# Linear attention with routed experts on one core: rows of tokens through the gate and up products in pairs, four places per pair for the attention's steps, loop transfers on GpSimd

## The chip, the cores and the metric

The kernel runs on one core of a Trainium2 chip. The metric is the device time of one execution, in microseconds; the time before is the median of three runs. Beside these there is one profiled execution, whose records all views of the profile come from.

## What is computed

The input x has 8 sequences of 1024 tokens with 256 features; everything is float32. After a layer norm without weights, two branches are added to x:

```python
q, k, v = (xn @ W.T for W in (Wq, Wk, Wv))          # 16 heads of 16
q, k = elu(q) + 1, elu(k) + 1
kv_cumsum = cumsum(einsum('blhd,blhe->blhde', k, v), axis=1)
out = einsum('blhd,blhde->blhe', q, kv_cumsum)
out = out / clip(einsum('blhd,blhd->blh', q, cumsum(k, axis=1)), 1e-6)
attn = out.reshape(8, 1024, 256) @ Wo.T

logits = xn @ Wr + br                                # 8 experts
w, e = top_k(logits, 2);  w = softmax(w)
h = silu(xn @ W1[e]) * (xn @ W3[e])                  # 256 -> 512
ffn = sum over the two experts of w * (h @ W2[e])    # 512 -> 256
result = x + attn + ffn
```

## The kernel before

The 8192 tokens are 16 blocks of 512. The kernel has three strands of work, written into one program.

**Routing.** Each block is loaded (`load_x`, tile xb), normalised, turned so that features lie on partitions (`turn`, tile xnT, stored to xnT_d in DRAM for the attention), and multiplied by Wr. Every four blocks `route` finds the two best experts of each token and the token's place in its expert's list. From the lists come 128-token rows, each of one expert: `first_batch` makes 25 rows (N1) from the first four blocks, `second_batch` makes 110 more (N2) when all blocks are routed. Each batch yields a table with the expert of each row (te_i), the token numbers to gather (src_i), and the numbers of the table entries (num_i). Of the 135 rows the last three (NR) run only if they are needed; 132 are run by the loop.

**Experts.** For one row j: `ffn_load` gathers its 128 tokens (tile xg) and their weights and norm factors (tile entry) with two indirect transfers on GpSimd; `ffn_weights` reads the expert's number into a register of SyncE and loads W1 and W3 of that expert, 512 KB each (tile w13; its pool has 5 buffers); `ffn_norm` normalises on ScalarE; `ffn_turn` transposes on TensorE into PSUM (xg_t) and copies to xgT; `ffn_hidden` does the gate and up products, each 4 x 2 products of 128 x 128 weights with 128 columns of tokens, into two PSUM tiles gu_ps; a Silu on ScalarE (L1147) and a product on VectorE (L1150) make hT; `ffn_out` multiplies with W2 (y_ps, 256 columns) and scales (L1165); `ffn_store` adds the result into DRAM with an indirect transfer. In float32 the profile shows each product as two records.

**Attention.** `block_steps` cuts each block into 11 steps: projections (zq, zkk, zkv), transposes of k (tp) and the running sum ksum on VectorE, the denominators (den, then two reciprocals on VectorE, L843), and for each of four chunks of 128 tokens the scores (s_ps, four PSUM tiles at once; masked on VectorE, L872), the state update (kv_ps), the weighting (o_ps) and the output projection (a_ps). `attend_upto(n)` advances this strand until n steps are made.

The loop runs over the rows. One pass of it: normalise row j + 1; in the first 12 passes route another block, whose transfers (load_x, and the store of xnT in `turn`) stand on ScalarE's queue; then `attend_upto`; then `ffn_step(j)`, which issues loads for rows ahead, does `ffn_hidden(j)`, `ffn_turn(j + 1)`, `ffn_out(j - 1)`, and the store. So the attention's steps, about 1.4 for a row in the late part, stand in one place per row, between the y products of one row and the gate products of the next.

Four PSUM tiles (pool ps_mm) serve zq, zkk, zkv, den, s_ps and gu_ps; two (ps_t) serve xg_t, tp, kv_ps and o_ps; two (ps_y) serve y_ps and a_ps. After the start, whose order is written out by hand, a scheduler puts the instructions of each engine into an order by its own estimate of times; the order of the built program can be read without running it.

Of the kernel before, what the change touches and what calls it, by code (L numbers as in the profile page):

```python
# [47 lines left out]
I32 = mybir.dt.int32  # L48
# [14 lines left out]
def tile_attention_moe(  # L63
# [33 lines left out]
    NM = NF - NR  # L97
    assert N2 <= P and N1 <= 32 and 2 * FT * N1 + 32 <= KC * TB
# [214 lines left out]
    def turn(t):  # L313
        xn = scaled.pop(t)
        if 0 < t < FB:
            xnT = e_one.tile([P, KC, TB], F32, name=f"xnT{t}")
        else:
            xnT = (two if t == 0 else f_two).tile([P, KC, TB], F32, tag="xnT", name="xnT")
        for k in range(KC):
            tp = ps_t.tile([P, TB], F32, tag="t", name="tp")  # L320
            for c in range(NCH):
                done = nc.tensor.transpose(
                    tp[:, bass.ts(c, P)], xn[:, c, bass.ts(k, P)], ident
                )
                if t == FB + 1:
                    in_order(done)
            nc.scalar.copy(xnT[:, k, :], tp)
        if t == 0:
            turned_first.append(xnT)
        else:  # L330
            last_store[0] = nc.scalar.dma_start(out=xnT_d[t], in_=xnT.rearrange("p k l -> p (k l)"))
        turned[t] = xnT
# [197 lines left out]
    def rows_of(past, jumps, room, start, n, name):  # L530


        nc.vector.tensor_tensor(
            jumps, past, room.unsqueeze(1).to_broadcast([P, n, E - 1]), ALU.mult
        )
        rows = f_one.tile([P, n], F32, name=name)
        nc.vector.tensor_reduce(rows, jumps, op=ALU.add, axis=AX.X)
        if start is None:
            nc.vector.tensor_tensor(rows, rows, cols[:, 0:n], ALU.add)
        else:  # L540
            nc.vector.scalar_tensor_tensor(
                rows, rows, start, cols[:, 0:n], ALU.add, ALU.add
            )
        return rows
# [53 lines left out]
    def first_batch():  # L598
# [17 lines left out]
        past = past_experts(upto, N1, e_one, "past")  # L616
        taken = f_one.tile([P, E], F32, name="taken")
# [7 lines left out]
        rows = rows_of(past, jumps, room, None, N1, "rows1")  # L625
# [15 lines left out]
        for j in range(2):  # L641
            for a in range(0, FT, PART):
                if j == 1 and a >= late:
                    at = late_at[(a - late) // PART]
                else:
                    at = at_places(place, j, a)
                for i in range(PART):
                    c = N1 * (j * FT + a + i)
                    nc.tensor.matmul(
                        sum_ps[32 * i : 32 * i + 32, :], lhsT=marks[:, c : c + 32],  # L650
                        rhs=at[:, i, :], start=(j + a == 0), stop=(j == 1 and a == FT - PART),
                        skip_group_check=True,
                    )
                if j == 0 and a == 2 * PART:
                    _, te_i = numbers_of(past, N1, "1")
            if j == 0:
                yield
# [9 lines left out]
    def second_batch(taken):  # L667
# [4 lines left out]
        upto = add_up(left, "upto2")  # L672
        past = past_experts(upto, N2, f_x, "xb")
        te, te_i = numbers_of(past, N2, "2")
        nc.vector.tensor_copy(rows_left, upto[0:1, E - 1 : E])

        room = f_one.tile([P, E - 1], F32, name="room2")
        nc.vector.tensor_scalar(
            room, rows[:, 0 : E - 1], -1.0, float(ROWS), ALU.mult, ALU.add
        )  # L680
        nc.vector.tensor_tensor(room, room, taken[:, 1:E], ALU.add)
        of_tiles = rows_of(past, past, room, taken[:, 0:1], N2, "rows2")
# [384 lines left out]
    ffn5 = ctx.enter_context(tc.tile_pool(name="ffn5", bufs=5))  # L1067
    ffn4 = ctx.enter_context(tc.tile_pool(name="ffn4", bufs=4))
    ffn8 = ctx.enter_context(tc.tile_pool(name="ffn8", bufs=8))
# [12 lines left out]
    def ffn_load(j):  # L1082
        table, _, num_i, src_i, _, _, i = of_tile(j)
        xg[j] = ffn4.tile([P, H], F32, tag="xg", name="xg")
        nc.gpsimd.indirect_dma_start(  # L1085
            out=xg[j], out_offset=None, in_=x_rows[:, :],
            in_offset=bass.IndirectOffsetOnAxis(ap=src_i[:, i : i + 1], axis=0),
        )
        entry[j] = ffn8.tile([P, 3], F32, tag="entry", name="entry")
        nc.gpsimd.indirect_dma_start(  # L1090
            out=entry[j], out_offset=None, in_=table[:, :],
            in_offset=bass.IndirectOffsetOnAxis(ap=num_i[:, i : i + 1], axis=0),
        )

    def ffn_norm(j):
        in_order(
            nc.scalar.activation(  # L1097
                xg[j], xg[j], AF.Identity, bias=entry[j][:, 1:2], scale=entry[j][:, 2:3]
            )
        )  # L1100

    def ffn_turn(j):

        tp = ps_t.tile([P, KC, P], F32, tag="t", name="xg_t")
        for k in range(KC):
            nc.tensor.transpose(tp[:, k, :], xg.get(j)[:, bass.ts(k, P)], ident)  # L1106
        xgT[j] = ffn2.tile([P, KC, P], F32, tag="xgT", name="xgT")
        nc.scalar.copy(xgT[j], tp)  # L1108
# [8 lines left out]
    def ffn_weights(j):  # L1117
        e = expert_of(j, mybir.EngineType.SP)
        for s, w in enumerate((w1, w3)):
            ws[j, s] = ffn5.tile([P, KC, I], F32, tag="w13", name="w13")  # L1120
            in_order(
                nc.sync.dma_start(
                    out=ws[j, s],
# [4 lines left out]
    def ffn_hidden(j, last=False):  # L1128


        gu = []
        for s in range(2):
            if last and s == 1:
                ffn_out(j - 1, True)
            w13 = ws.pop((j, s))
            ps = ps_mm.tile([P, IC, P], F32, tag="mm", name="gu_ps")
            for i in range(IC):
                for k in range(KC):
                    done = nc.tensor.matmul(  # L1139
                        ps[:, i, :], lhsT=w13[:, k, bass.ts(i, P)], rhs=xgT[j][:, k, :],  # L1140
                        start=(k == 0), stop=(k == KC - 1),
                    )
                    if last:
                        in_order(done)
            gu.append(ps)
        hT = ffn2.tile([P, IC, P], F32, tag="hT", name="hT")
        silu = nc.scalar.activation(hT, gu[0], AF.Silu)  # L1147
        if j == 0:
            in_order(silu)
        nc.vector.tensor_tensor(hT, gu[1], hT, ALU.mult)  # L1150
        hs[j] = hT

    def ffn_out(j, last=False):
        hT = hs.pop(j)
        e = expert_of(j, mybir.EngineType.PE)
        y_ps = ps_y.tile([P, H], F32, tag="y", name="y_ps")
        for i in range(IC):
            done = nc.tensor.matmul(  # L1158
                y_ps, lhsT=hT[:, i, :], rhs=w2_sb[:, bass.ds(e * (IC * H) + i * H, H)],
                start=(i == 0), stop=(i == IC - 1),  # L1160
            )
            if last:
                in_order(done)
        ys[j] = ffn5.tile([P, H], F32, tag="y", name="y")
        nc.vector.tensor_scalar(ys[j], y_ps, entry.pop(j)[:, 0:1], None, ALU.mult)  # L1165

    def ffn_store(j):
        _, _, _, _, rows, dst_i, i = of_tile(j)
        nc.gpsimd.indirect_dma_start(  # L1169
            out=rows[:, :],  # L1170
            out_offset=bass.IndirectOffsetOnAxis(ap=dst_i[:, i : i + 1], axis=0),
            in_=ys.pop(j), in_offset=None, compute_op=ALU.add,
        )

    stored = [0]

    def ffn_step(j, behind):


        if j + 3 < NM:  # L1180
            ffn_load(j + 3)
        if j + 2 < NM:
            ffn_weights(j + 2)
        if j < NM:
            ffn_hidden(j, j == NM - 1)
        if j + 1 < NM:
            ffn_turn(j + 1)
        if j > 0 and j != NM - 1:
            ffn_out(j - 1)
        for _ in range(2):  # L1190
            if stored[0] < j - behind:
                ffn_store(stored[0])
                stored[0] += 1


    for j in range(3):
        ffn_load(j)
    for j in range(2):
# [5 lines left out]
    LATE = 3  # L1204
# [3 lines left out]
    for j in range(NM + 1):  # L1208
        if j + 1 < NM:
# [5 lines left out]
        if j == 0:  # L1215
            for i in range(3, 6):
                load_x(t + i, nc.scalar)
        if 0 < j and t < NBLK:
# [6 lines left out]
            if t + 5 < NBLK:  # L1225
                load_x(t + 5, nc.scalar)
# [15 lines left out]
        if LISTS <= j < LISTS + NBLK - FB:  # L1242
            t = FB + j - LISTS
            rows = slice(t * TB, (t + 1) * TB)
            in_order(nc.sync.dma_start(out=out_rows[rows, :], in_=x_rows[rows, :]))
        if j < LISTS:
            attend_upto(3 + j // 2)
        elif j < READ:
            attend_upto(AHEAD - 2 * (READ - j - 1))
        else:  # L1250
            attend_upto(AHEAD + (NBLK * STEPS - AHEAD) * (j - READ + 1) // (NM - READ - 4))
# [3 lines left out]
        ffn_step(j, LATE if N1 < j <= N1 + LATE else 0)  # L1255
    while stored[0] < NM:
# [6 lines left out]
    with tc.If(used > N2 - NR):  # L1263
        for j in range(NM, NF):
            ffn_load(j)
# [3 lines left out]
            ffn_hidden(j)  # L1269
# [39 lines left out]
```

## Time and profile before

| | us |
|---|---|
| median of three runs | 1396.2 |
| lowest and highest | 1394.3, 1397.18 |
| profiled execution | 1388.92 |
| its span, first to last instruction | 1387.1 |
| TensorE (PE) busy in the span | 1328.5 |
| VectorE (DVE) busy | 728.0 |
| ScalarE (ACT) busy | 488.7 |
| GpSimd (POOL) busy | 528.3 |

The profiled execution is 7.3 us shorter than the median. Busy time is the time in which at least one instruction of the engine runs; PE is TensorE's products, PEld its weight loads, SP the engine that issues most transfers. In lists of groups and waits a line such as L1139 is the line of the kernel, "out<-in" are the program's tiles, and x is a count. A wait is written as "who, line <- whom, line: us in total, times, longest". In timelines the columns are start, duration, engine, line, operation, tiles, count, and in brackets the idle time before it and what ended it.

### The profile page before, as it was taken

The numbers are of one execution on the slowest core, as the hardware profiler recorded it, in microseconds if no ns is written. First come the engines' busy times: TensorE is split into PE (matmuls) and PEld (weight loads), VectorE is DVE, ScalarE is ACT, GpSimd is POOL, SyncE is SP. The second block draws the span as 40 slices with busy tenths as digits, with TensorE's granted clock in tenths as the row PEclk, the third lists the DMA queues.
The fourth block names the chain that finished last, engine by engine and source line by source line (L and its number), as shares of the span: only waits on it lengthen the run. The fifth ranks groups of instructions, "written<-read, shape, count | busy, mean of one in ns | idle before, by whom it ended". The sixth has DMA issues, their size and how long they took to land.

```text
span 1387.1 us, 27907 instructions
## 1 busy us (share of the span) xinstructions
PE 1328.5 (96%) x10906; PEld 1127.2 (81%) x10906; DVE 728.0 (52%) x1428; ACT 488.7 (35%) x914; POOL 528.3 (38%) x457
## 2 busy tenths in 40 slices
PE   5799999999999999999999999999999999999996
PEld 4578887878888888888888888888788788888895
DVE  7786589784353536354453536363544435363631
ACT  5466351141514233252525142342524151423321
POOL 3533332223334333434433333443434244334432
PEclk9999999999999999999999999999999999999999
DMA  9687653455756555555656555565647375555553
GB/s 346 236 275 234 180 169 109 120 143 145 211 160 152 164 124 145 150 145 151 152 147 164 147 151 152 140 173 139 162 129 175 109 173 160 132 164 138 147 151 80
DMA packets 129412, 223.56 MB, mean 161 GB/s; under 512 B 14818, under 2 KB 53346, under 8 KB 128994
## 3 DMA queue, kind: packets, MB, share of 16 engines
q1 hardware_dynamic: 84306, 165.95, 36.9%
q0 software_dynamic: 38064, 43.22, 19.3%
q10 hardware_dynamic: 6912, 12.58, 2.5%
q8 instruction: 90, 1.47, 0.4%
q14 instruction: 40, 0.33, 0.1%
HBM read 187.91 MB, written 44.29 MB: 167 GB/s over the span
## 4 chain that ended last, share of the span: by engine, by line
PE 82%; DVE 11%; ACT 3%; issue 2%; DMA 2%; POOL 0%; POOLq 0%; ACTq 0%; DVEq 0%
PE gu_ps L1139 32%; PE y_ps L1158 15%; PE s_ps L865 6%; PE o_ps L906 4%; PE a_ps L928 4%; PE zq L764 4%; PE zkk L780 3%; PE zkv L780 3%; PE kv_ps L880 2%; DVE rden L843 2%; PE xg_t L1106 2%; PE held_ps L696 2%; PE o_ps L899 2%; PE den L842 2%; DVE ksum L832 2%
## 5 line engine op out<-in xcount | busy, mean ns | idle before, releaser
L1139 PEld LDWEIGHTS gu_ps<-xgT,w 128*128 128x128 f32 x4224 | 494.7, 193 | 28.8 <-issue 17.2
L1139 PE MATMUL gu_ps<-xgT,w 128*128 128x128 f32 x4224 | 511.6, 278 | 2.3 <-DVE s_sb L872 1.9
L1085 POOL DMA_INDIRECT xg<-in_x_dram,src_i x132 | 129.8, 983 | 547.7 <-ACT xgT L1108 437.8
L1158 PE MATMUL y_ps<-w_sb,hT 128*128 x1056 | 251.9, 380 | 2.5 <-DVE hT L1150 1.3
L1169 POOL DMA_INDIRECT out_dram<-y,dst_i x107 | 173.6, 1622 | 159.4 <-DVE y L1165 85.1
L1150 DVE TENSOR_TENSOR hT<-gu_ps,hT 128x512 f32<-128x512 f32 x132 | 90.4, 685 | 248.2 <-PE gu_ps L1139 229.2
L1147 ACT ACTIVATE hT<-gu_ps 128x512 f32<-128x512 f32 x132 | 78.8, 597 | 381.1 <-PE gu_ps L1139 380.2
L1158 PEld LDWEIGHTS y_ps<-w_sb,hT 128*128 128x128 f32 x1056 | 190.0, 190 | 25.9 <-issue 2.6
L872 DVE TENSOR_TENSOR s_sb<-s_ps,causal 128x512 f32<-128x512 f32 x256 | 163.2, 683 | 73.6 <-PE s_ps L865 71.8
L1165 DVE TENSOR_SCALAR y<-y_ps,entry 128x256 f32<-128x256 f32 x132 | 63.7, 482 | 137.6 <-PE y_ps L1158 137.6
L1090 POOL DMA_INDIRECT entry<-tab_d,of_i x107 | 111.2, 1040 | 37.8 <-issue 31.7
L865 PE MATMUL s_ps<-qm,kT 32*128 32x256 f32 x1024 | 107.6, 412 | 3.4 <-DVE rden L843 2.0
L843 DVE RECIPROCAL rden<-den 128x512 f32<-128x512 f32 x32 | 105.4, 3329 | 3.4 <-PE den L842 3.4
L1108 ACT COPY xgT<-xg_t 128x256 f32<-128x256 f32 x132 | 49.0, 372 | 152.3 <-PE xg_t L1106 150.7
L865 PEld LDWEIGHTS s_ps<-qm,kT 32*128 32x128 f32 x1024 | 61.6, 185 | 39.1 <-issue 19.5
L933 ACT COPY at<-a_ps 128x256 f32<-128x256 f32 x64 | 23.8, 372 | 176.9 <-PE a_ps L928 176.7
L1097 ACT ACTIVATE xg<-xg,entry 128x256 f32<-128x256 f32 x132 | 79.6, 603 | 5.6 <-issue 5.6
L928 PE MATMUL a_ps<-wo_sb,oT 128*128 128x256 f32 x256 | 67.2, 384 | 5.7 <-DVE oT L914 5.6
L906 PE MATMUL o_ps<-s_sb,va 128*32 128x128 f32 x2048 | 71.8, 278 | 0.0
L764 PE MATMUL zq<-xnT,wq_sb 128*128 128x512 f32 x128 | 61.0, 609 | 0.0
L928 PEld LDWEIGHTS a_ps<-wo_sb,oT 128*128 128x128 f32 x256 | 47.0, 190 | 16.6 <-DVE oT L914 9.4
L1169 POOL DMA_INDIRECT acc_d<-y,src_i x25 | 44.0, 1761 | 42.2 <-DVE y L1165 30.7
(199 smaller groups left out, 1440.6 us busy)
## 6 DMA issues: line engine op xcount, KB each, us to landing
w<-in_w_dram SPq DMA_DIRECT2D x264, 512.0 KB, 4.4
xnT_d<-xnT ACTq DMA_DIRECT2D x15, 512.0 KB, 4.7
xnT<-xnT_d SPq DMA_DIRECT2D x15, 512.0 KB, 5.9
out_dram<-in_x_dram SPq DMA_DIRECT2D x12, 512.0 KB, 5.2
out_dram<-at POOLq DMA_DIRECT2D x12, 512.0 KB, 7.7
xb<-in_x_dram ACTq DMA_DIRECT2D x9, 512.0 KB, 6.0
w_sb<-in_w_dram SPq DMA_DIRECT2D x4, 1024.0 KB, 11.8
xb<-in_x_dram SPq DMA_DIRECT2D x7, 512.0 KB, 7.4
```

Source lines behind the costliest of these rows:

```text
L764: nc.tensor.matmul(z, lhsT=wq_sb[:, k, bass.ts(o, P)], rhs=xnTs[t][:, k, :], start=(k == 0), stop=(k == KC - 1),)
L843: nc.vector.reciprocal(rden[:, o, :], den)
L865: nc.tensor.matmul(s_ps[r][:, hh].rearrange("p a l -> p (a l)"), lhsT=kT[rows, hh, span], rhs=qm[rows, hh, :, span], start=True, stop=True,)
L872: nc.vector.tensor_tensor(sm, s_ps[r].rearrange("p k a l -> p (k a) l"), causal_b, ALU.mult)
L906: nc.tensor.matmul(o_ps[32 * r : 32 * r + 32, hh, :], lhsT=va[:, c, 4 * hh + r, a, :], rhs=s_sb[r][:, 2 * hh + a, :], start=(first and a = ...
L928: nc.tensor.matmul(a_ps, lhsT=oT[:, hh, :], rhs=wo_sb[:, hh, :], start=(hh == 0), stop=(hh == 1),)
L1085: nc.gpsimd.indirect_dma_start(out=xg[j], out_offset=None, in_=x_rows[:, :], in_offset=bass.IndirectOffsetOnAxis(ap=src_i[:, i : i + 1], a ...
L1090: nc.gpsimd.indirect_dma_start(out=entry[j], out_offset=None, in_=table[:, :], in_offset=bass.IndirectOffsetOnAxis(ap=num_i[:, i : i + 1], ...
L1139: done = nc.tensor.matmul(ps[:, i, :], lhsT=w13[:, k, bass.ts(i, P)], rhs=xgT[j][:, k, :], start=(k == 0), stop=(k == KC - 1),)
L1150: nc.vector.tensor_tensor(hT, gu[1], hT, ALU.mult)
L1158: done = nc.tensor.matmul(y_ps, lhsT=hT[:, i, :], rhs=w2_sb[:, bass.ds(e * (IC * H) + i * H, H)], start=(i == 0), stop=(i == IC - 1),)
L1169: nc.gpsimd.indirect_dma_start(out=rows[:, :], out_offset=bass.IndirectOffsetOnAxis(ap=dst_i[:, i : i + 1], axis=0), in_=ys.pop(j), in_off ...
```

## The change

Rows of the second batch whose expert has two or more of them are run in pairs. `second_batch` now lists 48 pairs first (two rows of one expert in places next to each other, 96 rows), then 14 single rows, of which 11 are run by the loop. The loop runs over units: 25 single rows of the first batch, 48 pairs, 11 single rows. For a pair:

- W1 and W3 are loaded once; the pool of w13 has 4 buffers instead of 5.
- The transposes of both rows go into one tile of 256 columns. The gate and up products have 256 columns, and the hidden part is done in two halves of 256 features: gate, up, Silu and product of the first half, then of the second. Each half's PSUM tile has the size of before.
- The attention's steps stand in four places: before the first half, between the halves, after the second half, and between the y products of the two rows. The goal of steps is spread over the four.
- Gathers, entries, scalings and stores remain one per row.

The stores of xnT for blocks after the fifth, and the loads of x in the loop, go from ScalarE's queue to GpSimd's. In `first_batch` the experts' numbers te_i of the first batch are made right after `past_experts`, and no longer among the list's products. `second_batch` has some fifteen more small operations on VectorE to count pairs.

```diff
+    ND = (2 * NT - N1 - E + 1) // 2
+    N2D = 2 * ND
...
-            last_store[0] = nc.scalar.dma_start(out=xnT_d[t], in_=xnT.rearrange("p k l -> p (k l)"))
+            queue = nc.scalar if t <= FB else nc.gpsimd
+            last_store[0] = queue.dma_start(out=xnT_d[t], in_=xnT.rearrange("p k l -> p (k l)"))
...
         past = past_experts(upto, N1, e_one, "past")
+        _, te_i = numbers_of(past, N1, "1")
...
-                if j == 0 and a == 2 * PART:
-                    _, te_i = numbers_of(past, N1, "1")
...
+        nc.vector.tensor_scalar(pairs_i, pairs_i, 1, None, ALU.arith_shift_right)
...
+        upto = add_up(pairs, "upto2")
+        nc.vector.tensor_scalar(upto, upto, float(ND), 2.0, ALU.min, ALU.mult)
...
-    ffn5 = ctx.enter_context(tc.tile_pool(name="ffn5", bufs=5))
     ffn4 = ctx.enter_context(tc.tile_pool(name="ffn4", bufs=4))
-    ffn8 = ctx.enter_context(tc.tile_pool(name="ffn8", bufs=8))
+    ffn12 = ctx.enter_context(tc.tile_pool(name="ffn12", bufs=12))
...
+    units = [(j,) for j in range(N1)]
+    units += [(j, j + 1) for j in range(N1, N1 + N2D, 2)]
+    units += [(j,) for j in range(N1 + N2D, NF)]
+    NU = len(units) - NR
...
+    def ffn_turn(u):
+        n = P * len(units[u])
+        tp = ps_t.tile([P, KC, n], F32, tag="t", name="xg_t")
...
-            ws[j, s] = ffn5.tile([P, KC, I], F32, tag="w13", name="w13")
+            ws[u, s] = ffn4.tile([P, KC, I], F32, tag="w13", name="w13")
...
+    def ffn_hidden(u, between, last=False):
+        n = P * len(units[u])
+        m = TB // n
+        hT = ffn2.tile([P, IC, 2 * P], F32, tag="hT", name="hT")[:, :, 0:n]
+        for a in range(0, IC, m):
+            if a > 0:
+                between()
+            gu = []
+            for s in range(2):
...
+                ps = ps_mm.tile([P, m, n], F32, tag="mm", name="gu_ps")
+                for i in range(m):
+                    for k in range(KC):
+                        done = nc.tensor.matmul(
+                            ps[:, i, :], lhsT=ws[u, s][:, k, bass.ts(a + i, P)],
+                            rhs=xgT[u][:, k, :], start=(k == 0), stop=(k == KC - 1),
+                        )
...
+            half = hT[:, a : a + m, :]
+            silu = nc.scalar.activation(half, gu[0], AF.Silu)
...
+            nc.vector.tensor_tensor(half, gu[1], half, ALU.mult)
...
+    def ffn_out(u, between=None, last=False):
...
+        for r, j in enumerate(units[u]):
+            if r > 0:
+                between()
+            y_ps = ps_y.tile([P, H], F32, tag="y", name="y_ps")
...
+        if u < NU:
+            ffn_hidden(u, between, u == NU - 1)
+        if u < NU and len(units[u]) > 1:
+            between()
+        if u + 1 < NU:
+            ffn_turn(u + 1)
+        if u > 0 and u != NU - 1:
+            ffn_out(u - 1, between)
...
-                load_x(t + 5, nc.scalar)
+                load_x(t + 5, nc.gpsimd)
...
-            attend_upto(AHEAD + (NBLK * STEPS - AHEAD) * (j - READ + 1) // (NM - READ - 4))
+            unit = units[min(j, NU - 1)]
+            n = 4 * len(unit) - 4 or 1
+            upto = [
+                AHEAD + (NBLK * STEPS - AHEAD) * (n * (unit[0] - READ + 1) + len(unit) * i)
+                // (n * (NM - READ - 4))
+                for i in range(n)
+            ]
+        goals = iter(upto)
+        attend_upto(next(goals))
...
+        ffn_step(j, LATE if N1 < j <= N1 + LATE else 0, lambda: attend_upto(next(goals, 0)))
```

## The prediction

> **What bounds the kernel now.** I read the page first: busy shares, then slices.
>
> ```profile
> PE 1328.5 (96%) x10906; PEld 1127.2 (81%) x10906; DVE 728.0 (52%) x1428; ACT 488.7 (35%) x914; POOL 528.3 (38%) x457
> PE   5799999999999999999999999999999999999996
> PEclk9999999999999999999999999999999999999999
> DMA  9687653455756555555656555565647375555553
> L1139 PE MATMUL gu_ps<-xgT,w 128*128 128x128 f32 x4224 | 511.6, 278 | 2.3 <-DVE s_sb L872 1.9
> ```
>
> PE is busy 96% of the span at nearly full clock; no other engine passes 52%. It idles in the first two slices and the last. So the end moves only by what shortens PE's stream or the waits in it. A product's record (278 ns) is longer than its step, as products overlap; the step comes from starts. The timeline of PE near the end, where nothing stands between the steps:
>
> ```profile
> 1350.75 3.73 PE L1139 MATMUL gu_ps<-xgT,w 128*128 128x128 f32 x32
> 1354.32 0.38 PE L1106 MATMUL xg_t<-ident,xg 128*128 128x128 f32 x2
> 1354.54 1.89 PE L1158 MATMUL y_ps<-w_sb,hT 128*128 x8
> 1356.27 3.73 PE L1139 MATMUL gu_ps<-xgT,w 128*128 128x128 f32 x32
> ```
>
> From start to start, 32 gate and up records of 128 columns take 3.57 us, 111.6 ns each; 8 records of y_ps, 256 columns each, take 1.73 us, 216 ns each. Weight loads are already nearly hidden.
>
> Next the waits of weight loads between 250 and 1340 us, where PE loses time to data:
>
> ```profile
> PEld den L842 <- DVE ksum L837: 11.0, 14, 1.5
> PEld a_ps L928 <- DVE oT L914: 8.7, 10, 1.3
> PEld s_ps L865 <- ACT va L797: 7.0, 14, 0.5
> PEld s_ps L865 <- DVE rden L843: 3.6, 4, 0.9
> ```
>
> They are few and short: the long list of steps is already well interleaved. Last, the timeline of the start:
>
> ```profile
> 43.35 1.23 POOL L1090 DMA_INDIRECT entry<-tab_d,num_i  x1 [4.20 <-DVE at_i L589]
> 44.89 0.98 POOL L1085 DMA_INDIRECT xg<-in_x_dram,src_i  x1 [0.30 <-PE zkv L780]
> 50.95 0.60 ACT L1097 ACTIVATE xg<-xg,entry 128x256 f32<-128x256 f32 x1 [5.63 <-issue]
> 51.61 0.44 PE L1106 MATMUL xg_t<-ident,xg 128*128 128x128 f32 x2 [4.39 <-ACT xg L1097]
> ```
>
> PE waits 4.39 us for the first gathered row.
>
> **Part 1, products of 256 columns.** The built program has 48 pairs. A pair today is 64 records x 111.6 ns = 7.14 us; as 32 records at y_ps's step, 216 ns, it is 6.91 us. 48 x 0.23 = 11 us less, all on PE, which is the path. Bounds: nothing (if w as the loaded side holds a record at 2 x 111.6) and 11.7 (finer starts). I take 11, since y_ps, zkk and zkv all step at 216.
>
> The Trainium skill, "TensorE: Matmul & The Clock Gate", section "Back-to-back issue gap", gives a sustained spacing of about 81 ns for 128 columns and 131 ns for 512, so that wide products would be far cheaper per column; interpolated, an estimate, a pair would save 40%, over 100 us. The rows here, 111.6 and 216 ns, are almost proportional to columns, so the sum doesn't use it.
>
> **Part 2, the places.** Before, attention steps stood in one place per row, after y's products; now also between the halves of the hidden products, after them, and between the two y's. I count neighbours in the two built orders on PE and price each by rows.
>
> Taken out:
> - Scores straight after scores: 5 before, 2 after, and the second set waits for four masks (L872), 0.61 us apart: 1.5 us each. With one that keeps only xg_t between (1.1), -3.5.
> - Scores after den and zkv with nothing else: 5 before, 1 after. In the timeline s_ps runs from 536.61 to 540.08, 3.47 us for a usual 1.07; 0.8 of it is the ACT copy of va and stays, as zkv before s_ps counts 15 in both. 4 x 1.6 = -6.5, and -2.6 for the two gu that such a pile-up delayed (5.36 us instead of 3.7 in one).
> - a_ps straight after its own o_ps and scores: waits of up to 1.3 us on oT; five such before, one after: -4. Two more a_ps and y's that came too early: -4.
>
> Sum -20.6.
>
> Put in:
> - s_ps straight after gu: none before, 12 after. Scores need all four mm buffers, and the last holds the up product until L1150 has read it. The end of the run shows that wait: 16 records from 1370.82 end their steps at 1372.61, y_ps starts at 1373.62 "[0.85 <-DVE hT L1150]", 1.0 us lost. s_ps behind va loses 0.8. I take 0.93: +11. Bounds 0.8 and 1.3.
> - xg_t straight after kv_ps and o_ps: none before, 11 after. Both tiles of ps_t are then held; at 706.24 kv is read for 0.42 us, when o_ps has ended at 706.45: 0.3 each, +3.3. Bounds 0 and 0.7.
> - a_ps after only 1.73 us of y (9 times): oT was ready 4.8 us after s_ps began, PE would come at 4.9; 0.25 each, +2.3 (0 to 0.5).
> - tp after zkk with 2.2 to 2.6 us between, four times; before, gu, xg_t and y lay there, 5.5 us. 0.5 each, +2 (0 to 1.3).
> - den after tp: three are better covered and four worse. +2 (-2 to +9), nearest row den <- ksum.
>
> Sum +20.6: the places give and take the same.
>
> **Part 3, the start.** te_i (L525, L527: 0.33 + 0.20 us on DVE) was at 39.18 and comes some 5.8 us earlier; SP then waits for tab's store, which issued at 35.00, so the weights issue near 36 and not 39.97. DVE's chain to the lists has the same operations in another order: nothing. In the DMA view of 39 to 54 us five weight loads (2.5 MB) fill the engines at some 385 GB/s from 41.3 to 48.5, and the entry gathers there land in 5.8 us, where the page has 3.1. After, with four w13 buffers, 2 MB are through at about 43, and the gather of 44.89 (done 45.87, landing 2.7 us) is there at 48.6: -2.5. Bounds 0 and -3.7.
>
> The Trainium skill, "DMA: Bandwidth & Descriptors", section "Queues, rings and completion order", says that a DMA engine goes round its queues packet by packet. By that the gathers wouldn't have queued behind the weights and the gain would be near nothing; the landing of 5.8 us differs from that, so I keep -2.5.
>
> **Part 4, the moved transfers.** ACT loses 20 issues (0.35 to 0.5 us, off the path: ACT 35%). POOL gets them at 1.4 us (row L938, the same 512 KB shape), 28 us between 50 and 160 us where it is busy three tenths. Behind each xnT_d store, which waits for ACT's copy, stand the gather of the row three later and a store; rows take 8 us, so two rows cover it: 0. Without that cover it costs 1.4 us a row, 15 us; I take 0.
>
> In the paired stretch POOL has per pair two gathers, two entries, two stores (2 x (1.25 + 1.3 + 1.9)) and about 4 us for a store's landing that the next awaits: 13 of some 20 us. 0, and if it passed 20, each us more would be PE's.
>
> **Part 5, small.** w13 has 4 buffers instead of 5: w for a unit goes out when the products of the one two before are done, at least 9 us ahead; it lands in 4.4 us median, 11.9 at most. 0. The extra count operations on DVE near 165 us, about fifteen of 0.17 to 0.25 us, lie among the lists that PE waits for: +0.5 (0 to 3). The 90 SP loads fewer (264 to 174): 0, as none is waited for. The tail is the same order: 0.
>
> **Sum.** -11 - 20.6 + 20.6 - 2.5 + 0.5 = -13. The waits taken out were priced one by one, and some lie behind each other, so I give 2 us back: -11. The profiled execution took 1388.9 us (span 1387.1 and 1.8 around it) and would be 1377.9. The median of the runs shown, 1396.2, is 7.3 us over it; the same difference gives 1385.
>
> **Rivals.** A measurement of this kernel tells 0.2% (2.8 us) from no change.
> 1. Slower: the four mm buffers become the limit. If L1150 stands behind masks or reciprocals, each of the 12 s_ps after gu and 11 xg_t after o_ps costs more. For it: DVE takes its operations in the order written, and the two reciprocals after den hold it for 6.57 us. Against: DVE is 52% busy. It decides where those 23 places cost 11 us more in all, 1.1 us each instead of 0.62; at 1.5 each it is +20: 1405.
> 2. Faster by more: the order lets buffers come free in time, and the places cost 8 rather than 20.6: 1372. For it: the built order moves y and xg_t into most gaps.
> 3. The wide product doesn't step at 216 ns: part 1 is 0, 1396.
>
> **Chances.** Forecast 0.55 (own range 1377 to 1394), rival 1 0.22, rival 2 0.15, rival 3 0.08. Faster: 0.52 + 0.15 + 0.01 = 0.68; slower 0.22; same 0.10. The lower end takes the low bounds of part 2 with a start of -3.7, about 1370; the upper end goes two thirds of the way to all high bounds together (part 2 +21, the start and the lists +2.5 each, +26), 1403.
>
> **What would show it.** Right: gu records of 128x256 stepping at 216 ns; the first xg_t near 49 us; s_ps waiting on hT about 0.9 us a dozen times; den and a_ps waits as before. Wrong: PE idle above 60 us, waits of s_ps or xg_t over 1 us many times, ACT or PE waiting for xg, entry or w, or a gu step of 223 ns.

## The result, and the profile after

The changed kernel takes 1417.25 us (median of 5 runs, 1415.14 to 1421.42) for 1396.86 before: a ratio of 1.0154, interval 1.0131 to 1.0177. It is slower by 20 us. The forecast was 1385, its range 1370 to 1403. The profiled execution took 1421.42 us, span 1419.7.

All runs below were made in series, each on one chip beside the kernel before; that took 1396 us in two series (the result's and one other) and 1386 to 1389 us in the other five, so times are compared within a series, or as ratios to the kernel before.

From the page of the changed kernel: engines, slices, the largest group.

```profile
PE 1329.9 (94%) x9370; PEld 1073.8 (76%) x9370; DVE 727.0 (51%) x1443; ACT 488.7 (34%) x872; POOL 539.0 (38%) x477
...
PE   5778999998999999999999999999999999999995
...
PEclk9888999999999999999999999999999999999998
...
L1183 PE MATMUL gu_ps<-xgT,w 128*128 128x256 f32 (+1 forms) x2688 | 491.4, 337 | 0.5 <-ACT xgT L1147 0.5
```

The products do what they should: gu_ps is busy 20 us less than before (511.6). But PE, at 9 tenths from the third slice on before, now stands at 7 in the third and 8 in the fourth, and the granted clock is down in the second to fourth slice: 35 to 142 us, where the loop over x runs. Landmarks in the traces (start of y's products of a row, us; e10 and e11 are runs that come below) say where time is lost:

```
                              row 0   row 10   row 26   row 130      end
before                         68.6    160.7    375.2    1369.1   1387.1
after (the result)             74.0    187.0    405.2    1397.7   1419.7
after, another series (e11)    65.3    175.1    386.3    1368.6   1389.5
loads moved back (e10)         63.2    157.9    369.1    1349.6   1367.8
```

Of the 33 us between the first two traces 5 are there by row 0 and 26 by row 10; from row 10 to row 130, with all the pairs, they are 2 us apart. The execution traced for the kernel before (1388.92 us) is shorter than every timed run of its series, so these 33 us hold more than the change. The last two lines are from one chip: they differ in the queue of the nine x loads alone, and of their 22 us 2 are there by row 0 and 17 by row 10.

**How the loop loses it.** GpSimd's and ScalarE's own timelines, first after, then before (start, us, engine, line; in brackets the idle time and what ended it):

```profile
100.56 0.60 POOL L335 DMA_DIRECT2D xnT_d<-xnT  x1
101.14 0.84 POOL L148 DMA_DIRECT2D xb<-in_x_dram  x1
114.82 1.01 POOL L1115 DMA_INDIRECT xg<-in_x_dram,src_i  x1 [12.85 <-PE xg_t L1145]
117.08 1.64 POOL L1219 DMA_INDIRECT acc_d<-y,src_i  x1 [1.25 <-DVE y L294]
119.02 1.00 POOL L1120 DMA_INDIRECT entry<-tab_d,num_i  x1 [0.30 <-issue]
120.01 0.60 POOL L335 DMA_DIRECT2D xnT_d<-xnT  x1
120.58 0.85 POOL L148 DMA_DIRECT2D xb<-in_x_dram  x1
```

```profile
101.45 0.35 ACTq L331 DMA_DIRECT2D xnT_d<-xnT  x1
101.84 0.45 ACTq L145 DMA_DIRECT2D xb<-in_x_dram  x1
...
108.95 0.34 ACTq L331 DMA_DIRECT2D xnT_d<-xnT  x1
109.34 0.46 ACTq L145 DMA_DIRECT2D xb<-in_x_dram  x1
```

On GpSimd four issues stand between one row's x load and the next: a gather that waits for a row to be turned (12.85 us here), a y store that waits for VectorE, an entry, and an xnT_d store, which needs ScalarE's copy. 19.4 us pass between the two loads shown here (blocks 13 and 14), 7.5 between those shown of before (14 and 15); blocks 13 and 14 were 12.5 us apart there. From block 10's load to block 15's it is 63.4 us after and 42.5 before. What waits for the load is VectorE, and behind it TensorE (VectorE's and TensorE's timelines of after):

```profile
102.11 0.43 DVE L275 BATCH_NORM_STATS2 st<-xb 128x6 f32<-128x256 f32 x1 [4.50 <-DMA xb<-in_x_dram]
...
103.06 0.16 DVE L292 TENSOR_TENSOR sq<-sq,half 128x8 f32<-128x8 f32 x1
```

```profile
103.21 0.80 PE L431 MATMUL cnt_ps<-both,upto_neg 128*128 128x128 f32 x2 [5.13 <-DVE sq L292]
```

TensorE's wait is put down to sq, a tiny operation; sq stood behind the statistics of x. The clock falls with the gap. Windows of 10 us, after and before (PE, PEld, DVE, ACT, POOL busy, then the granted clock):

```profile
100.00:110.00 10.00, 6.79 (x40) 4.83 (x41) 5.85 (x28) 1.55 (x2) 1.97 (x3) 0.58 0.62 210
```

```profile
100.00:110.00 10.00, 10.00 (x102) 8.20 (x102) 5.58 (x28) 6.37 (x15) 3.70 (x4) 1.00 0.93 273
```

The clock was granted at 0.5 for 28 us between 50 and 200 us, for 3.4 us before. TensorE was busy in 21 of the 28 us. In the trace of before, gate and up products that had 0.5 for 3.4 us took 1.6 us longer than their 3.73 (540.64 us, shown under Part 1 below), so about half of such time is lost: an estimate of 11 us here and 2 before. The clock fell at 101.7 us, 1.5 us before this gap ended, and stayed down until 111.9 us; by the same estimate the gap of 5.1 us cost some 4 us more.

### The profile page after: what moved, and what is told of

It reads as the page before. It is cut to its first block, busy times and chain, and to the rows that moved or that the text cites. A ratio compares the mean times of both kernels' runs of the same rounds, so it can differ in the third digit from the quotient of the medians.

```text
span 1419.7 us, 24110 instructions
## 1 busy us (share of the span) xinstructions
PE 1329.9 (94%) x9370; PEld 1073.8 (76%) x9370; DVE 727.0 (51%) x1443; ACT 488.7 (34%) x872; POOL 539.0 (38%) x477
## 4 chain that ended last, share of the span: by engine, by line
PE 76%; DVE 10%; ACT 6%; issue 4%; DMA 2%; POOL 1%; another core or an unknown queue 1%; POOLq 0%; DVEq 0%; ACTq 0%
PE gu_ps L1183 28%; PE y_ps L1206 13%; PE s_ps L896 5%; PE o_ps L937 4%; PE a_ps L959 4%; PE zkv L811 4%; PE zq L795 3%; PE zkk L811 2%; PE kv_ps L911 2%; PE den L873 2%; PE xg_t L1145 2%; PE held_ps L727 2%; PE o_ps L930 2%; DVE ksum L863 1%; DMA xb<-in_x_dram 1%
## 5 line engine op out<-in xcount | busy, mean ns | idle before, releaser
L1183 PE MATMUL gu_ps<-xgT,w 128*128 128x256 f32 (+1 forms) x2688 | 491.4, 337 | 0.5 <-ACT xgT L1147 0.5
L1183 PEld LDWEIGHTS gu_ps<-xgT,w 128*128 128x128 f32 x2688 | 427.4, 192 | 57.5 <-issue 15.2
L1147 ACT COPY xgT<-xg_t 128x512 f32<-128x512 f32 (+1 forms) x84 | 41.4, 493 | 144.4 <-PE xg_t L1145 143.2
L959 PE MATMUL a_ps<-wo_sb,oT 128*128 128x256 f32 x256 | 67.3, 385 | 10.2 <-DVE oT L945 10.2
L1134 ACT ACTIVATE xg<-xg,entry 128x256 f32<-128x256 f32 x132 | 74.0, 597 | 1.1 <-DVE mv L276 1.1
```

What stands on the lines that cost most here:

```text
L959: nc.tensor.matmul(a_ps, lhsT=oT[:, hh, :], rhs=wo_sb[:, hh, :], start=(hh == 0), stop=(hh == 1),)
L1183: done = nc.tensor.matmul(ps[:, i, :], lhsT=ws[u, s][:, k, bass.ts(a + i, P)], rhs=xgT[u][:, k, :], start=(k == 0), stop=(k == KC - 1),)
```

## The experiments

**Which transfers.** Each moves loads (`load_x`) or stores (`xnT_d`) between `nc.gpsimd` and `nc.scalar`, nothing else; one series.

```diff
     stores: e1, e3
-            queue = nc.scalar if t <= FB else nc.gpsimd
-            last_store[0] = queue.dma_start(...)
+            last_store[0] = nc.scalar.dma_start(...)
     loads, in two places: e1, e2
-                load_x(..., nc.gpsimd)
+                load_x(..., nc.scalar)
     e4: the kernel before, with both edits the other way, to nc.gpsimd
```

> The changed kernel with the loop's x loads and xnT_d stores back on ScalarE's queue; all else as changed. Theory Q (queue): on GpSimd's queue these transfers stand behind gathers that wait for TensorE, x comes late, and by the eleventh row the changed kernel is 26 us behind (row 10's y at 187.0 us for 160.7). So here row 10's y comes near 161 to 163 and the time falls by some 26 us to 1388 to 1394. Rival S (start): the earlier count of experts and the weights that go out sooner are what upsets the loop; then row 10 stays near 185 and the time near 1415. Rival P (pairs): the loss is spread over the pairs; then row 10 is right but the time stays above 1405.

> The changed kernel with only the loop's x loads back on ScalarE's queue; the xnT_d stores stay on GpSimd's. Theory Q: the loads are what VectorE waits for (xb: 20.4 us in 5 waits), so most of the loss goes: 5 to 8 us above the run with both moved back. If instead the stores hold the xnT buffers (ScalarE waits 6.5 us for them), half or more of the loss stays: 12 us above or more. Rival S or P: no change against the changed kernel, about 1417.

> The changed kernel with only the xnT_d stores back on ScalarE's queue; the x loads stay on GpSimd's. Theory Q with the loads as the cause: 10 to 20 us above the run with both moved back, 1400 to 1412. With the stores as the cause: within 5 us of it. Rival S or P: about 1417.

> The kernel before with only the loop's x loads and xnT_d stores moved to GpSimd's queue. Theory Q: the transfers alone make the loss; row 10's y moves from 160.7 to 180 or later, time 1415 to 1423. With 8 entry buffers instead of 12, some 4 entry gathers fewer (1.25 us each) go out ahead of the first store, so the loss may be 5 us smaller. Rival S or P: within 3 us of the kernel before, 1394 to 1400.

```
                                     time     ratio to before (1388.16)
e1 loads and stores back           1375.72    0.9907 [0.9881, 0.9932]
e2 loads back                      1373.99    0.9898 [0.9868, 0.9929]
e3 stores back, loads on GpSimd    1387.47    0.9992 [0.9980, 1.0005]
e4 before, both on GpSimd          1408.32    1.0152 [1.0125, 1.0179]
```

The move alone costs the kernel before 20 us (e4). The stores alone on GpSimd cost nothing (e2 against e1); the loads alone there cost 12 (e3 against e1). Both there cost 18 to 20 (e11 and e13 below), which suggests that a store ahead of a load is not free. VectorE's waits between 50 and 190 us, of e4, e3 and e10 in this order, show the same:

```profile
DVE st L272 <- DMA xb<-in_x_dram: 16.9, 4, 6.3
```

```profile
DVE st L275 <- DMA xb<-in_x_dram: 19.1, 6, 4.7
```

```profile
DVE st L275 <- DMA xb<-in_x_dram: 1.7, 2, 1.0
```

Before it was 4.6 us in 3 waits. The loads of block 12 of x, from the traces: the first transposition of block 7, whose buffer it takes; its issue; its first statistics.

```
                     block 7 turned   load issued   first statistics   in all
e10 loads back            75.5            76.6            81.2            5.7
before                    77.0            80.9            87.7           10.7
e3 loads on GpSimd        77.9            86.3            93.3           15.4
e11 after                 76.9            84.4            92.9           16.0
e4 before, on GpSimd      77.5            84.5            93.7           16.2
```

For this block it is 4.6 us from issue to use where the load is alone on ScalarE's queue, and 6.8 to 9.2 elsewhere; where GpSimd issues it, 7 to 8.4 us are lost before the issue. Rows 2 to 4, in which this block is due, take 20 us in the first two and 27 in the others.

The Trainium skill, "DMA: Bandwidth & Descriptors", section "SWDGE vs HWDGE vs iDMA", gives plain transfers to the queues of SP or ACT and leaves GpSimd the irregular ones. The runs agree on the outcome. The reason given there, a faster set-up, is seen in the issue (0.45 us for 0.84) but is not what cost the time: the median landing of an x load was 5.6 and 6.2 us from GpSimd (e3, e11) and 5.0 to 6.0 from ScalarE (e2, e1, before); what is left is the place in the queue.

**On one chip.** The changed kernel and the loads moved back (e2's kernel), side by side in two series, and the latter alone in two more.

> The run with the loads moved back to ScalarE once more, beside the changed kernel on one chip, since the two stood in different series (0.990 and 1.015 to 1.020, on chips on which the kernel before took 1388 and 1396 us). Theory Q (the loads' place on GpSimd's queue costs 26 us or more): 25 to 40 us below the changed kernel, ratio 0.988 to 0.995. Rival C (part of that difference lies in the chip): 20 us or less below it.

> The changed kernel beside the run with the loads moved back. Theory Q: ratio 1.015 to 1.022. If in this series too oT waits up to 3.2 us beside GpSimd's stores, the paired stretch from row 26 to row 130 takes 992 to 996 us; without that wait 982 to 985.

> The changed kernel, beside the three others of this series. If the series is like the first (kernel before at 1396 us): ratio 1.015 to 1.021, oT held beside GpSimd's stores four times by 1.7 us or more. If like the second (1388 us): 1.002 to 1.006, oT never held.

> The run with the loads moved back. Theory Q: whatever the series, 17 to 20 us (1.3%) below the changed kernel, as many as row 10 is earlier (157.9 for 175.1 us): ratio 1.002 to 1.008 in a series like the first, 0.987 to 0.992 in one like the second. Rival: in a series like the first the loss is not the transfers at all but the wait beside GpSimd's stores; then it stays within 8 us of the changed kernel there.

> The run with the loads moved back, for a series like the first, if this is one. There, by the transfers' price alone (18 us): ratio 1.002 to 1.008. If the wait beside GpSimd's stores does not come with the loads moved back: 0.988 to 0.995. In a series like the second again: 0.988 to 0.993.

> As in the run before: in a series like the first, 1.002 to 1.008 by the transfers' price alone, 0.988 to 0.995 if the wait beside GpSimd's stores does not come with the loads moved back; in a series like the second, 0.988 to 0.994.

```
                        changed kernel                       loads moved back
e11, e10     1393.09   1.0040 [1.0019, 1.0061]      1374.64   0.9895 [0.9867, 0.9924]
e13, e14     1392.15   1.0038 [1.0020, 1.0057]      1372.06   0.9910 [0.9883, 0.9937]
e17                                                 1376.56   0.9932 [0.9910, 0.9954]
e18                                                 1376.62   0.9913 [0.9878, 0.9948]
```

The loads' place costs 18 and 20 us, not the 25 to 40 that I expected of theory Q: my rival C was right that part of the distance between series lay elsewhere. In these series the changed kernel is 0.4% slower, not 1.5.

**In a series with 1396 us.** The changed kernel again; a version that breaks up the queue on GpSimd; and the entry ring of before.

> The changed kernel itself, for a trace from the same chip as the other runs. Ratio to the kernel before about 1.015. In its first profile rows 26 to the end took 1014.5 us, in the run with only the loads moved back 1001.0, though TensorE's list is the same there. If that is a difference between two executions, it will be near 1001 to 1004 here; if it follows from the loop, near 1014 again.

> The changed kernel with both loop transfers still on GpSimd, but in the first twelve units each row's gathers are issued one row later and behind the loads and stores of that step, so the gather's buffer is long free and no transfer stands behind a gather that waits for TensorE, nor behind the run of early entry gathers. Theory Q1 (waiting behind gathers is the cause): most of the loss goes, row 10's y at 158 to 168, ratio 0.988 to 0.998. Rival Q2 (GpSimd's own issuing, 0.6 to 0.85 us a transfer, or a slower way to memory): row 10 stays at 180 or later, ratio 1.01 or more.

> The changed kernel with 8 entry buffers as before, not 12. In the changed kernel seven entry gathers of 1.25 us each go out in a row ahead of the first xnT_d store (63.4 to 70.6 us). With 8 buffers four fewer go ahead: if these count, the first store issues near 65.6 and the time falls by 5 us or somewhat more where a stall also lowers the clock, ratio 1.008 to 1.012. If only the later waits behind the gathers count: 1.014 to 1.017.

```diff
e6  -while loaded[0] < min(u + 4, NU) and ...
    +while loaded[0] < min(u + (3 if u < LISTS else 4), NU) and ...
     ...
    +    if u < LISTS:
    +        with tc.issue_after((last_x[0] if u < 8 else last_store[0]).ins):
    +            ffn_load(j)
     ...
e7  -tile_pool(name="ffn12", bufs=12)
    +tile_pool(name="ffn12", bufs=8)
```

e5: 1422.78 us, 1.0205 [1.0174, 1.0237]. e6: 1431.10, 1.0243 [1.0206, 1.0279]. e7: 1413.78, 1.0123 [1.0088, 1.0158]. Row 10 came at 182.6, 181.6 and 183.5 us.

e6 missed, and it doesn't decide between Q1 and Q2. The gathers no longer wait (xb waits fell to 8.3 us), but GpSimd now waited for y before acc_d's stores, up to 10.7 us with the loads behind them, and ScalarE waited 18.9 us for entries that were asked for a row later. One wait at the head of the queue was exchanged for another. e7's gain is not the loop's: row 10 is no earlier. Its trace gains in rows 18 to 20 (29.1 us for 36.4), where e5 had a wait of 3.6 us and a lowered clock.

Rows 26 to 130 took 996.1 us in e5 and 982.3 in e13, the same program on another chip. What differs is VectorE beside GpSimd's issues. Timelines of e5, then of e13:

```profile
605.87 1.61 POOL L1219 DMA_INDIRECT out_dram<-y,dst_i  x1 [0.30 <-issue]
...
607.79 0.98 POOL L1120 DMA_INDIRECT entry<-tab_d,of_i  x1 [0.30 <-issue]
...
609.17 0.42 DVE L945 SCALAR_TENSOR_TENSOR oT<-rden,o_ps 128x256 f32<-128x256 f32 x1 [4.11 <-PE y_ps L1206]
...
609.65 0.70 PE L959 MATMUL a_ps<-wo_sb,oT 128*128 128x256 f32 x2 [1.73 <-DVE oT L945]
```

```profile
590.37 1.61 POOL L1219 DMA_INDIRECT out_dram<-y,dst_i  x1 [0.30 <-issue]
...
590.56 0.42 DVE L945 SCALAR_TENSOR_TENSOR oT<-rden,o_ps 128x256 f32<-128x256 f32 x1 [1.00 <-PE o_ps L937]
```

In both o_ps is complete 0.1 us after the store's issue begins. In e13 oT starts 0.07 us later, in e5 3.2 us later, after GpSimd's two issues. It happened in all five traces of the two series with 1396 us and in no other; a_ps waits 11.4 us for oT in e5 and 1.5 in e13.

The start of the loop has the like, and longer. In e5 GpSimd issues one transfer after another until 69.77 us, at most 0.3 us apart. TensorE, VectorE and ScalarE there, and VectorE in e13:

```profile
62.59 0.49 PE L1183 MATMUL gu_ps<-xgT,w 128*128 128x128 f32 x2
64.00 0.43 PE L344 MATMUL lg_ps<-xnT,wr_sb 128*32 128x128 f32 x8 [0.92 <-issue]
70.67 0.69 DVE L1194 TENSOR_TENSOR hT<-gu_ps,hT 128x512 f32<-128x512 f32 x1 [8.75 <-remote]
70.74 0.27 ACT L349 COPY lgT<-lg_ps 128x128 f32<-128x128 f32 x1 [6.79 <-remote]
```

```profile
65.20 0.69 DVE L1194 TENSOR_TENSOR hT<-gu_ps,hT 128x512 f32<-128x512 f32 x1 [1.60 <-PE gu_ps L1183]
```

gu_ps is complete at 63.1 us and lg_ps at 64.4, but hT and lgT start 7.6 and 6.3 us later ("remote" is a release whose sender the trace doesn't show). In e13 hT starts with its data, beside the same issues. So 5 of the 6 us by which e5 is behind e13 at row 10 are there by row 0; the result's trace, too, has an idle time of 8.5 us on VectorE there.

**Places and start**, on the kernel with the loads moved back: two places per pair (e8, e15), three (e12, e16), and te_i at its old place (e9).

```diff
e8   -            if a > 0:
     -                between()
     ...
     -            if r > 0:
     -                between()
     ...
     -            n = 4 * len(unit) - 4 or 1
     +            n = 2 * len(unit) - 2 or 1
e12  -        if u < NU and len(units[u]) > 1:
     -            between()
     ...
     +            n = 3 * len(unit) - 3 or 1
e9   -        _, te_i = numbers_of(past, N1, "1")
     ...
     +                if j == 0 and a == 2 * PART:
     +                    _, te_i = numbers_of(past, N1, "1")
```

> The run with the loads moved back to ScalarE, with two places per pair (before the first half and after the second) instead of four: as many places per row as before the change. My forecast priced the four places at nothing, -20.6 and +20.6. If that holds, the ratio stays within 0.003 of 0.990. If the places gain (less piling up of attention steps), it rises by 0.005 to 0.015; if the put-in waits weigh more than those taken out, it falls by as much.

> Two places per pair, with the loads moved back. If the price of 4% (1.0335 for about 0.990) is the places': 30 us or more above the run with the loads moved back here too. If part of it came from the slower series: 15 to 25 us above it, as its rows 26 to 130 took 34 us more than in the run with the loads moved back, of which gu_ps 8, s_ps 18, and 5 in products that cost 0 to 1 elsewhere.

> The run with the loads moved back, with three places per pair: the one after the second half is left out, where twelve sets of scores came straight after the products and seventeen xg_t straight after o_ps (now 7 and 2). My forecast priced these two at 0.93 and 0.3 us a time: then the 5 and 15 fewer give back 4.7 and 4.5 us, 9 us, ratio near 0.983. The traces show 0.09 us a time for both (309 for 216 ns, 203 for 112 ns): then 1 to 2 us, and what the lost place piles up elsewhere decides, ratio 0.988 to 0.997.

> Three places per pair, with the loads moved back (0.9861 in the second series for 0.9895 with four). If three are better than four: 3 to 6 us below the run with the loads moved back. If the two are the same: within 2 us.

> The run with the loads moved back, with the first count of experts (te_i) at its old place. My forecast gave the early count 2.5 us (0 to 3.7): then this run is 2 to 4 us slower than the one with the loads moved back, and its first xg_t is near 51.5 us for 49. If weights and gathers share the engines so that the order of issue is no matter: no difference, within 1.5 us.

```
e8   two places      1440.10   1.0335 [1.0299, 1.0371]   series with 1396
e15  two places      1386.79   1.0013 [0.9997, 1.0029]   e14, four: 0.9910
e12  three places    1370.97   0.9861 [0.9833, 0.9889]   e10, four: 0.9895
e16  three places    1369.97   0.9890 [0.9866, 0.9914]   e14, four: 0.9910
e9   te_i late       1373.55   0.9888 [0.9860, 0.9916]   e10, early: 0.9895
```

Two places cost 15 us beside four (e15 against e14), not the 60 that e8 suggests: the two traces are 50 us apart, 14 of them by row 0, where ScalarE stood for 13.2 us in e8, and 32 in rows 26 to 130. Three beat four by 4 and 2 us, with intervals that overlap; three with the loads moved back is the best version run and beats both kernels. For the early count the timed runs show nothing (1 us, intervals of 4 us each way); the first xg_t came at 48.8 us in e10 and 50.8 in e9.

## Why the prediction was wrong

**Part 4, the moved transfers: 0 forecast, 18 to 20 us measured.** This is the step that failed. I asked what stands behind an xnT_d store and answered gathers and stores, covered by two rows. The x loads were moved too, and I did not ask what stands ahead of them: in the new order a gather, a y store, an entry and an xnT_d store, each with its own wait. Nor did I ask how long a load may be late. The trace of before held it: block 12's statistics began 6.8 us after its issue, and VectorE already waited for x three times. There was no cover. The price I named without it, 1.4 us a row for the issue, was of the wrong thing: an issue took 0.6 to 0.85 us, and the traces show the loss in waits, with a lowered clock beside them. That those 15 us lie near the measured 18 to 20 is luck. With Part 4 at 19 the sum would have been +8 for -11; the two series that hold the changed kernel at 1392 to 1393 us show +4 to +5.

**The rest of the sum held.** Parts 1, 2, 3 and 5 gave -11; with the loads moved back the five ratios of 0.9895 to 0.9932 are -10 to -15 us. The sum held in part by luck, as its terms show. TensorE's time from row 26 to row 130, each product's step charged to its kind (us):

```
          gu_ps   y_ps   s_ps    o2   a_ps   tp    others   sum
before    378.7  186.3   85.6   52.6  47.3  12.0   231.4   993.9
e10       362.6  193.7   80.2   53.6  46.4  13.9   230.2   980.6
```

**Part 1: right.** The wide records step at 216 ns; in e10, 16 of them take 3.45 us to the next product:

```profile
562.56 3.62 PE L1183 MATMUL gu_ps<-xgT,w 128*128 128x256 f32 x16
566.01 0.60 PE L1145 MATMUL xg_t<-ident,xg 128*128 128x128 f32 x4
```

gu_ps falls by 16, of which 11 were forecast as steps and 2.6 as gu's delayed in pile-ups. I misread these 2.6: both gu stood at a lowered clock. The first of them, in the timeline of before, and the window of its start:

```profile
540.64 5.36 PE L1139 MATMUL gu_ps<-xgT,w 128*128 128x128 f32 x32
540.00:544.00 4.00, 4.00 (x21) 3.92 (x21) 2.06 (x5) 0.00 (x0) 0.00 (x0) 0.58 0.00 0
```

The other took 4.72 us at 620.48, with the clock at 0.5 from 619.1 to 622.5. e10's trace has no such stretch in these rows, so up to 3.4 of the 13 us between the two lines of the table are the clock's.

**Part 2: wrong in its terms, which cancel.** y_ps +7.4, tp +1.9 and o2 +1.0 stand against s_ps -5.4 and a_ps -0.9 and gu's remainder: give and take of about 10 each, where I had 20.6. The largest put-in was sized ten times too high: scores straight after gu, 0.93 us a time, cost 0.09 (309 ns for a step of 216), since VectorE had read the up product almost in time (e2's trace, as the next three). TensorE's waits of e10 from 250 to 1340 us:

```profile
PE s_ps L896 <- DVE hT L1194: 2.6, 12, 0.2
```

Twelve of them, as counted, but 0.2 us each. I had taken the price from the run's end, where nothing lies between. xg_t straight after o_ps made its weight loads wait 3.0 us for kv, but the products only 0.9, for 3.3; a_ps straight after its scores gave back 4 to 5 for 4; den lost 3.4 more than before (2 forecast for den after tp). That four places are needed at all, I had not priced: two cost 15 us.

**Part 3, the start: right in most traces, not in the times.** The first xg_t came at 51.6 us before. With the early count it came at 48.1 to 50.0 us in twelve traces, which is -1.6 to -3.5 for -2.5, and at 51.8 in five, the result's among them, which gained nothing. In all five the clock was at 0.5 from 40.2 to 50.5 us, in none of the twelve for more than 3.4 us in that time; what let it fall was not found.

**Part 5: 0.** The loads of w fell from 264 to 168, not to the 174 that I wrote. Rows 10 to 26 took 211.2 us in e10 and 214.5 before; but 211.3 in e4, which has the old lists. The 3 us are a lowered clock in the trace of before (0.89 granted from 300 to 330 us).

**The rivals.** The changed kernel came out slower, as rival 1 had it, but not by its mechanism: the mm buffers were in time (0.2 us a wait). Of my signs of being wrong one appeared, "PE idle above 60 us": 89.8 us, for 58.6 before.

**What stays open.** In the two series with 1396 us the changed kernel loses another 16 to 23 us against the kernel before. Between e5 and e13, 28 us apart, 6 are there by row 10 (5 by row 0), 7 fall in rows 18 to 20 (scores wait 3.6 us for masks, again beside GpSimd's issues, and the clock drops) and 14 in rows 26 to 130; the kernel before is itself 8.5 us slower there. Why VectorE and ScalarE are held there and not elsewhere was not found, and the version with only the loads moved back never ran in such a series, so that it beats the kernel before is shown for the other five alone; e8, which has the loads moved back too, ran in one, and there oT and ScalarE were held as well. No experiment put the loads on GpSimd with nothing waiting ahead of them; that the wait at the queue's head is the whole cost is read from the traces.

## What to carry to other kernels

Before moving a transfer to another queue, list what stands ahead of it there and what each of these waits for, and take from the trace how soon the data is used after its issue; a queue of transfers that nobody waits for can take a store, not a load that is used as it lands, and a store ahead of such a load may have its price too. When TensorE waits for a small operation, look at what that operation stood behind. And compare runs on one chip: between chips the same pair of kernels differed by 0.4% and by 2%.

## What was not expected of the hardware

With a gap of 5.1 us in TensorE's stream came 10.2 us at a granted clock of 0.5, of which 8.7 lay behind it. The length of a gap does not tell how long the clock stays down: behind 4.4 us of idle time in the trace of before (47.2 to 51.6 us) it was down for 3.4 us, and in e17 10.2 us followed a stretch in which TensorE was idle for 1.2 of 3.3 us (84 to 87.3 us).

In two series VectorE's oT, which reads one operand from SBUF and one from PSUM, was held up to 3.2 us beside GpSimd's DMA issues; in five series it started without such a wait (0.07 us after its data in e13) beside the same issues. The Trainium skill, "SBUF — State Buffer", section "Who interferes with whom", lets a VectorE instruction with at most one SBUF input, outside its two-port modes, run free of GpSimd. The five series agree with that. In the two, VectorE was held, and so was ScalarE, up to 13.2 us (e8); no run here tells why.
